# Moving beta and g of a gated delta rule into the feed-forward stage, and its closing norms into the rule's schedule

## The chip, the cores and the metric

The kernel runs on one core of a Trainium2 chip. The metric is the device time of one execution in microseconds (us); where several executions were timed, their median is given. Profiles are of one execution each. Engine names: PE is TensorE (matmuls; PEld its weight loads), DVE is VectorE, ACT is ScalarE, POOL is GpSimd, SP is SyncE, which issues most DMA transfers here.

## The reference, cut to what matters

The program is a decoder of two layers on 2048 tokens (32 sequences of 64, 256 features), all in float32: retention-like attention, banded cross attention, a feed-forward, then a gated delta rule, cross attention, and a mixture of 64 experts. A layer norm follows each. The change lies at the feed-forward of the first layer and the delta rule behind it:

```python
y = square(relu(x @ up)) @ down + (x @ expert) * sum_of_top2(x @ gate)
x = layernorm(x + layernorm(y) * gamma + beta)                    # feed-forward

beta = sigmoid(x @ w_b)                                           # [tokens, 32 heads]
g = -exp(a_log) * softplus(x @ w_a + dt_bias)                     # [tokens, 32 heads]
g = cumsum(g within each sequence)
decay[i, j] = exp(g[i] - g[j]) for i >= j                          # per sequence and head
...                                                               # the rule, 16 key heads, 32 value heads
x = layernorm(x + rule(x, beta, decay) @ w_out)
```

beta and g depend on nothing but the x that leaves the feed-forward.

## The kernel before, in words

The tokens are 16 tiles of 128, held in SBUF as `x[:, t, :]` throughout, and worked in four chunks of four tiles (512 tokens). One stage follows another; each has its own pools, and a tool that builds the program interleaves the instructions of neighbouring stages on each engine where their dependences let it.

The feed-forward (lines 662 to 708) is a plain loop over the four chunks. For a chunk it transposes x (`make_xT`, line 152: 8 transposes into two PSUM banks, two copies on ACT, L161), multiplies by the up weights in 8 blocks (`ph`, L678), takes relu on ACT (`hr`, L682, two buffers) and squares on POOL (`hT`, L683), then for each of the four tiles multiplies by the expert and gate weights (`pe`, L689) and the down weights (`py`, L692), and adds them on DVE (L694 to L700). Then a norm of y, the scaling on POOL (L705, L706), the addition to x (L707), and a norm of x (`layernorm`, L163: statistics on DVE, the power on POOL, four DVE operations L176). All PSUM tiles of the stage share one ring of 8 banks.

The delta rule's stage (from line 711) first loads constants by SP's queue (L718 to L760), among them two zero fills of the DRAM buffers `tudram` (L755, 1040 KB each, from a zeroed tile). It transposes x again for all four chunks (L742). Then it computes beta and g for all 16 tiles at once (lines 762 to 806): `pba` is x times w_b and w_a (L770, two groups of 8 tiles), ACT and DVE turn it into beta (exp, add, reciprocal) and into g (abs, exp, Ln, and three DVE operations), `pc` is the cumulative sum by a triangular matrix `tri` (L791, to `gall`), `pgT` the same transposed (L798), copied by ACT and stored by 16 DMA transfers to `gdram` (L804). The tiles of this part lie in a pool of their own, whose space the rule's working tiles take over.

The rule then has 64 steps, one for each of 16 key heads and 4 chunks: `conv` (projection `pp` L850, and a convolution over time on DVE, L859), `decay` for two steps (reloads g from `gdram` by a broadcast, L873; POOL subtracts, L884, L885; ACT exp, L888), `matrices` (`pn` L910, `pk` L943, stores to `adram` L957, and a reload `w` L964), `invert` (a triangular inverse on DVE, L1007, through `tudram`), `delta`, `gate` (`pz` L1047), `value` (`pv` L985), `output`, and `project` (L1158 to L1169), which adds to x.

Their order is not written by hand. Each of these is a Python generator, which yields steps such as `("pe", 1.75, "+")`: an engine, an estimated cost in us, and how many PSUM banks it takes (`+`) or gives back (`-`). `scheduled` (line 41) runs all streams in a model of the engines while the program is being built, and always emits next the step that can start first, with the streams' rank deciding among near equals. `("need", key)` holds a generator until another one has yielded `("set", key)`, which may add a latency. Streams come with the number of their items that may be under way. The emitted order is then fixed: on the chip each engine takes its instructions strictly in that order and waits on semaphores.

After the schedule four norms follow (lines 1199 to 1206), each with a store of its chunk of x to `xq`, from which the next stage, the second cross attention, loads its queries (`quarters`, L593).

Of the kernel before, what the change touches and what calls it, by code (L numbers as in the profile page):

```python
# [9 lines left out]
FP = mybir.dt.float32  # L10
# [8 lines left out]
P = 128  # L19
# [101 lines left out]
def decoder_kernel(ctx: ExitStack, tc: tile.TileContext, d, out):  # L121
# [537 lines left out]
        softmax_attention(wp, sb, ps, prologue, epilogue, True)  # L659


    with tc.tile_pool(name="f0", bufs=1) as wp, tc.tile_pool(name="f0w", bufs=2) as sb, tc.tile_pool(
        name="f0p", bufs=8, space=PSUM
    ) as ps:
# [7 lines left out]
        for c in range(NCH):  # L672
            make_xT(c, ps)
            hT = sb.tile([P, 8, 512], FP, name="hT", tag="hT")
            for f in range(8):
                ph = ps.tile([P, 512], FP, name="ph", tag="ps")
                for k in range(2):
                    nc.tensor.matmul(  # L678
                        ph, up[:, k, f * P : (f + 1) * P], xT[c][:, k, :], start=k == 0, stop=k == 1
                    )  # L680
                hr = sb.tile([P, 512], FP, name="hr", tag="hr")
                nc.scalar.activation(hr, ph, AF.Relu)  # L682
                nc.gpsimd.tensor_tensor(hT[:, f, :], hr, hr, ALU.mult)  # L683
            ys = []
            for k4 in range(4):
                cols = slice(k4 * P, (k4 + 1) * P)
                pe = ps.tile([P, D + 8], FP, name="pe", tag="ps")
                for k in range(2):
                    nc.tensor.matmul(pe, xT[c][:, k, cols], eg[:, k, :], start=k == 0, stop=k == 1)  # L689
                py = ps.tile([P, D], FP, name="py", tag="ps")  # L690
                for f in range(8):
                    nc.tensor.matmul(py, hT[:, f, cols], down[:, f, :], start=f == 0, stop=f == 7)  # L692
                m8 = sb.tile([P, 8], FP, name="m8", tag="m8")
                nc.vector.max(out=m8, in_=pe[:, D : D + 8])  # L694
                sc = sb.tile([P, 1], FP, name="sc", tag="sc")
                nc.vector.tensor_tensor(sc, m8[:, 0:1], m8[:, 1:2], ALU.add)
                ye = sb.tile([P, D], FP, name="ye", tag="ye")
                nc.scalar.activation(ye, pe[:, :D], AF.Copy, scale=sc)
                y = sb.tile([P, D], FP, name="y", tag=f"y{k4}")
                nc.vector.tensor_tensor(y, py, ye, ALU.add)  # L700
                ys.append(y)
            layernorm(ys, ys)
            tiles = [x[:, 4 * c + k4, :] for k4 in range(4)]
            for xt, y in zip(tiles, ys):
                nc.gpsimd.tensor_tensor(y, y, gam, ALU.mult)  # L705
                nc.gpsimd.tensor_tensor(y, y, bet, ALU.add)  # L706
                nc.vector.tensor_tensor(xt, xt, y, ALU.add)  # L707
            layernorm(tiles, tiles)


    with tc.tile_pool(name="g1", bufs=1) as wp, tc.tile_pool(
# [12 lines left out]
        PITCH = 65 * S  # L724
        adram = [dp.tile([2, 2, 8, PITCH], FP, name=f"adram{i}") for i in range(2)]
        tudram = [dp.tile([2, 2, 2, 8, PITCH], FP, name=f"tudram{i}") for i in range(2)]
        gdram = dp.tile([16, NCH, 2, 4, 2, S], FP, name="gdram")
        gall = wp.tile([P, NT, 32], FP, name="gall")

        wo16 = [wp.tile([P, 2, 16, 16], FP, name=f"wo16{i}") for i in range(2)]  # L730
        xis = [[wp.tile([P, 8, S], FP, name=f"xi{l}{i}") for i in range(2)] for l in range(2)]
# [7 lines left out]
        half = wp.tile([P, 4], FP, name="half")  # L739
        nc.gpsimd.memset(half, 0.5)  # L740

        for c in range(NCH):  # L742
            make_xT(c, ps)


        beta = wp.tile([P, NT, 32], FP, name="beta")
        with tc.tile_pool(name="g1l", bufs=1) as tmp:
            lvlf = load(tmp, d["c_lvl"].rearrange("p (l i) -> p l i", l=2), [P, 2, S], "lvlf")
            nc.vector.tensor_copy(lvl, lvlf)
# [4 lines left out]
            for t in tudram:  # L754
                nc.sync.dma_start(  # L755
                    out=t.rearrange("o c n u x -> (o c n u x)").rearrange("(p y) -> p y", p=P), in_=zero
                )
            tri = load(tmp, d["c_tri"], [P, P], "tri")
            wba = load(tmp, d["w_ba"].rearrange("(k p) e -> p k e", p=P), [P, 2, 64], "wba")
            dtb = load(tmp, d["dt_bias"].to_broadcast([P, 32]), [P, 32], "dtb")  # L760
            alog = load(tmp, d["a_log"].to_broadcast([P, 32]), [P, 32], "alog")
            g = tmp.tile([P, NT, 32], FP, name="g")
            aa = tmp.tile([P, NT, 32], FP, name="aa")
            ab = tmp.tile([P, NT, 32], FP, name="ab")
            for t8 in range(2):
                pba = ps.tile([P, 8, 64], FP, name="pba", tag="ps")
                for k8 in range(8):
                    t = 8 * t8 + k8
                    for k in range(2):
                        nc.tensor.matmul(  # L770
                            pba[:, k8, :], xT[t // 4][:, k, (t % 4) * P : (t % 4 + 1) * P], wba[:, k, :],
                            start=k == 0, stop=k == 1,
                        )
                sl = slice(8 * t8, 8 * t8 + 8)
                nc.scalar.activation(beta[:, sl, :], pba[:, :, 0:32], AF.Exp, scale=-1.0)
                nc.vector.tensor_tensor(aa[:, sl, :], pba[:, :, 32:64], over(dtb, 8), ALU.add)
            nc.vector.tensor_scalar(beta, beta, 1.0, None, ALU.add)
            nc.vector.reciprocal(beta, beta)
            nc.scalar.activation(alog, alog, AF.Exp)
            nc.scalar.activation(ab, aa, AF.Abs)  # L780
            nc.scalar.activation(ab, ab, AF.Exp, scale=-1.0)
            nc.scalar.activation(ab, ab, AF.Ln, bias=1.0)
            nc.vector.scalar_tensor_tensor(ab, aa, 0.0, ab, ALU.max, ALU.add)

            for hh in range(2):
                nc.vector.scalar_tensor_tensor(
                    g[:, :, 16 * hh : 16 * hh + 16], ab[:, :, hh::2], -1.0, over(alog[:, hh::2], NT),
                    ALU.mult, ALU.mult,
                )
            pc = pstile("pc")  # L790
            nc.tensor.matmul(pc, tri, g.rearrange("p t h -> p (t h)"), start=True, stop=True)  # L791
            nc.vector.tensor_copy(gall.rearrange("p t h -> p (t h)"), pc)

            gT = tmp.tile([32, NCH, 4, 2, S], FP, name="gTall")
            for c in range(NCH):
                pt = ps.tile([32, 4, P], FP, name="pgT", tag="ps")
                for k4 in range(4):
                    nc.tensor.matmul(  # L798
                        pt[:, k4, :], g[:, 4 * c + k4, :], tri, start=True, stop=True
                    )  # L800
                nc.scalar.copy(gT[:, c].rearrange("h t n i -> h (t n i)"), pt.rearrange("h t i -> h (t i)"))
                for n in range(2):
                    for hh in range(2):
                        nc.sync.dma_start(  # L804
                            out=gdram[:, c, n, :, hh, :], in_=gT[16 * hh : 16 * hh + 16, c, :, n, :]
                        )

        sb = stage.enter_context(tc.tile_pool(name="g1w", bufs=2))
        wsrc = d["w_qkv"].rearrange("(k p) e -> p k e", p=P)
# [21 lines left out]
        def conv(s, i):  # L831
# [3 lines left out]
            if i == first:  # L835
                yield "need", ("done", s - (5 if i == 2 or c == 0 else 6))
                yield "need", ("value" if i else "matrices", s - 2)
                if i == c == 0:
                    load_weights(kh)
                name = "vv" if i else "kq"  # L840
                projected[s, i] = sb.tile([P, 2, 512], FP, name=name, tag=name)
                yield "set", ("begun", s, i)
            else:
                yield "need", ("begun", s, first)
            dst = projected[s, first][:, 1 - i if i < 2 else i - 2]
            ct = (kh, 16 + kh, 32 + 2 * kh, 33 + 2 * kh)[i]
            yield "pe", 1.75, "+c"
# [19 lines left out]
        def decay(m):  # L867

            kh, c0 = steps[2 * m]
            yield "need", ("matrices", 2 * m - 3)  # L870
            de = sb.tile([P, 2, 8, S], FP, name="de", tag="de")
            for n in range(2):
                nc.sync.dma_start(  # L873
# [161 lines left out]
        def gate(s, h):  # L1035

            kh, c = steps[s]
            if h == 0:
                yield "need", ("done", s - 3)
                gates[s] = sb.tile([P, 2, 512], FP, name="z", tag="z", bufs=3)  # L1040
            yield "pe", 1.75, "+"
            if h == c == 0:
# [131 lines left out]
        def convs():  # L1174

            for m in range(-2, NS // 2):
# [3 lines left out]
                for s in (2 * m + 4, 2 * m + 5):  # L1180
                    if s < NS:
                        yield from (conv(s, 0), conv(s, 1))

        each = range(NS)
        scheduled(
            [
                ((output(s) for s in each), 1),
                ((matrices(s) for s in each), 2),
                ((value(s) for s in each), 1),
# [3 lines left out]
                (convs(), 2),  # L1193
                ((gate(s, h) for s in each for h in range(2)), 1),
                ((invert(m) for m in range(NS // 2)), 1),
            ],
            (6, 2), [(key, s) for s in range(-8, 0) for key in ("done", "matrices", "value", "output")],
        )
        for c in range(NCH):
            tiles = [x[:, 4 * c + k4, :] for k4 in range(4)]  # L1200
            layernorm(tiles, tiles)
            nc.sync.dma_start(
                out=xq[4 * c * P : (4 * c + 4) * P, :].rearrange("(t p) f -> p t f", p=P),
                in_=x[:, 4 * c : 4 * c + 4, :],
            )


    with tc.tile_pool(name="x1", bufs=1) as wp, tc.tile_pool(name="x1w", bufs=2) as sb, tc.tile_pool(
# [305 lines left out]
```

## Time and profile before

| what | us |
|---|---|
| median of 7 executions | 3573.0 |
| lowest and highest of them | 3568.04, 3584.35 |
| profiled execution, its own time | 3581.11 |
| its span, first to last instruction | 3579.4 |
| PE busy | 3311.9 (93%) |
| DVE busy | 2104.2 (59%) |
| POOL busy | 1525.2 (43%) |
| ACT busy | 1381.8 (39%) |
| feed-forward, first up matmul | 739.40 |
| the rule, first projection | 933.44 |
| the rule, last addition to x | 2597.75 |

The profile gives, for one execution, each engine's busy time, a strip of 40 slices of the span with the busy share in tenths, the granted clock of TensorE, and tables of instructions. In a row of the timeline the first number is the start in us from the beginning of the span, the second the length of a run of like instructions, then engine, line, operation, and what it writes and reads; `x32` is a count. A matmul of float32 appears as two passes, a transpose as one. In square brackets stands how long the engine had been idle and what ended it. "SPq" rows are DMA issues on SP's queue; they show the issue, not the transfer.

### The profile page before, as it was taken

What the parts mean: (1) busy time and instruction counts of PE and PEld (TensorE: products, weight loads), DVE (VectorE), ACT (ScalarE), POOL (GpSimd) and SP (SyncE); (2) the same over time, 40 slices, a digit from 0 to 9 for tenths busy, and PEclk for the clock granted to TensorE, in tenths of its full rate; (3) what the DMA queues carried; (4) which work ended last, traced back from release to release, by engine and by line L of the source; (5) the groups of instructions that cost most, each with busy time, mean ns of one, the idle gap of its engine ahead of it and who ended that gap; (6) DMA issues with size and microseconds to landing.
All of it is one profiled execution on the core that took longest, in us unless ns stands there. A gap on an engine that the chain in (4) does not pass through costs nothing.

```text
span 3579.4 us, 91942 instructions
## 1 busy us (share of the span) xinstructions
PE 3311.9 (93%) x39042; PEld 2137.0 (60%) x39042; DVE 2104.2 (59%) x4316; ACT 1381.8 (39%) x2422; POOL 1525.2 (43%) x1779
## 2 busy tenths in 40 slices
PE   9999999988799999999999999999979999699990
PEld 4667566655466666666676666666745555355550
DVE  4333566535476667777677677777567766233337
ACT  1110233322444455555455555555423333233330
POOL 3222344435334434444444444444334544466663
PEclk9999999999799999999899999999989998899995
DMA  9910111001242223323333233332221111466655
GB/s 313 384 49 13 43 31 31 27 31 38 52 78 55 57 55 70 64 55 57 62 60 66 57 67 63 62 59 48 46 49 53 63 49 41 163 220 211 214 176 217
DMA packets 538699, 317.80 MB, mean 89 GB/s; under 512 B 420144, under 2 KB 498736, under 8 KB 531888
## 3 DMA queue, kind: packets, MB, share of 16 engines
q1 hardware_dynamic: 517680, 259.32, 27.9%
q0 software_dynamic: 18432, 50.49, 3.9%
q8 instruction: 308, 5.05, 0.6%
q10 hardware_dynamic: 2176, 2.10, 0.2%
q14 instruction: 103, 0.84, 0.1%
HBM read 166.42 MB, written 137.00 MB: 85 GB/s over the span
## 4 chain that ended last, share of the span: by engine, by line
PE 77%; DVE 9%; POOL 5%; issue 4%; ACT 3%; DMA 1%; SPq 1%; POOLq 0%; DVEq 0%; ACTq 0%
PE pp L850 11%; PE py L1158 6%; PE po L531 6%; PE pz L1047 5%; PE pq L296 4%; PE pm L1067 4%; PE sc L467 3%; PE po L1118 3%; PE px L1067 3%; PE py L384 3%; PE sc L499 3%; PE py L1372 3%; PE pg L1362 2%; PE pu L1362 2%; PE ptu L1067 2%
## 5 line engine op out<-in xcount | busy, mean ns | idle before, releaser
L859 DVE SCALAR_TENSOR_TENSOR acc<-pp,cw,acc 128x504 f32<-128x504 f32 (+2 forms) x768 | 556.8, 731 | 195.2 <-ACT acc L854 165.3
L850 PE MATMUL pp<-xT,wqkv 128*128 128x512 f32 x1024 | 506.1, 620 | 22.5 <-DMA wqkv<-in_w_qkv_dram 11.7
L509 ACT ACTIVATE eT<-sc 128x768 f32<-128x768 f32 (+1 forms) x256 | 220.8, 914 | 265.7 <-PE sc L499 265.7
L903 POOL TENSOR_TENSOR sq<-kq 128x512 f32<-128x512 f32 x128 | 134.2, 1050 | 440.8 <-ACT kq L864 336.1
L204 POOL DMA_INDIRECT ybuf<-ye,xe x256 | 245.6, 959 | 176.8 <-DVE ye L1376 96.6
L477 DVE TENSOR_REDUCE mext<-sc 128x4 f32<-128x768 f32 (+1 forms) x256 | 267.3, 1087 | 73.1 <-PE sc L467 72.8
L850 PEld LDWEIGHTS pp<-xT,wqkv 128*128 128x128 f32 x1024 | 185.6, 194 | 185.1 <-issue 167.6
L1169 POOL TENSOR_TENSOR x<-x,y 128x256 f32<-128x256 f32 x256 | 184.2, 726 | 254.2 <-DVE x L1167 247.5
L854 ACT ACTIVATE acc<-pp,cw 128x512 f32<-128x512 f32 x256 | 175.2, 686 | 237.0 <-PE pp L850 236.3
L1158 PE MATMUL py<-wo,og 128*128 128x256 f32 x1024 | 259.2, 392 | 2.4 <-DVE x L1167 2.4
L1047 PE MATMUL pz<-xT,wz 128*128 128x512 f32 x512 | 246.2, 602 | 0.0
L518 POOL TENSOR_SCALAR_AFFINE_SELECT eT<-eT 128x256 f32<-128x256 f32 (+1 forms) x256 | 127.2, 531 | 201.3 <-ACT eT L509 201.3
L1158 PEld LDWEIGHTS py<-wo,og 128*128 128x128 f32 x1024 | 186.4, 192 | 43.6 <-issue 16.7
L467 PE MATMUL sc<-k,q 32*128 32x192 f32 (+1 forms) x2048 | 198.6, 397 | 10.6 <-DMA q<-xq 6.8
L1365 DVE TENSOR_TENSOR hT<-hT,pu 96x512 f32<-96x512 f32 x64 | 43.7, 683 | 238.1 <-PE pu L1362 221.9
L1167 DVE SCALAR_TENSOR_TENSOR x<-py,ro,x 128x256 f32<-128x256 f32 x256 | 122.4, 480 | 93.2 <-ACT y L1165 91.1
L499 PE MATMUL sc<-qb,k 32*128 32x192 f32 (+1 forms) x2048 | 160.5, 379 | 13.2 <-DVE mext L477 10.0
L1144 POOL TENSOR_TENSOR ro<-gvar,mhalf 128x8 f32<-128x8 f32 x64 | 105.2, 1644 | 147.5 <-DVE gvar L1139 137.8
L1165 ACT ACTIVATE y<-py,ro 128x256 f32<-128x256 f32 x256 | 120.4, 473 | 110.6 <-PE py L1158 101.6
L531 PE MATMUL po<-eT,va 128*32 128x192 f32 (+1 forms) x2048 | 159.9, 382 | 3.3 <-ACT eT L509 2.1
L298 DVE TENSOR_TENSOR tmp<-pq,cs 128x1024 f32<-128x1024 f32 x80 | 98.0, 1225 | 98.7 <-PE pq L296 93.9
L467 PEld LDWEIGHTS sc<-k,q 32*128 32x128 f32 x2048 | 116.2, 192 | 65.8 <-issue 36.2
(226 smaller groups left out, 6558.9 us busy)
## 6 DMA issues: line engine op xcount, KB each, us to landing
xbuf<-zero SPq DMA_DIRECT2D x32, 1032.0 KB
xe<-xbuf SPq DMA_DIRECT2D x64, 516.0 KB
tu<-tudram SPq DMA_DIRECT2D x256, 128.0 KB
ybuf<-zero SPq DMA_DIRECT2D x16, 1024.0 KB
de<-gdram SPq DMA_DIRECT2D x64, 256.0 KB
adram<-am SPq DMA_DIRECT2D x128, 128.0 KB
yk<-ybuf SPq DMA_DIRECT2D x16, 1024.0 KB
kk<-kT SPq DMA_DIRECT2D x32, 256.0 KB
```

Of the source, the lines that this page charges most:

```text
L204: i = nc.gpsimd.indirect_dma_start(out=dst, out_offset=bass.IndirectOffsetOnAxis(ap=rows, axis=0), in_=src, in_offset=None).ins
L467: nc.tensor.matmul(sc[ng // 2][:, ng % 2, qt * W : (qt + 1) * W], q32[rows, r, qt * P : (qt + 1) * P], k32[rows, r, lo[qt] : lo[qt] + W], ...
L477: nc.vector.tensor_reduce(mv4[:, 2 * hf : 2 * hf + 2, :, 8], sc[hf][:, :, : 2 * W].rearrange("p j (q l) -> p j q l", l=W), AX.X, ALU.max, ...
L499: nc.tensor.matmul(sc[ng // 2][:, ng % 2, lt * W : (lt + 1) * W], k32[rows, r, lt * P : (lt + 1) * P], qb[rows, lo[lt] : lo[lt] + W], star ...
L509: nc.scalar.activation(eT[:, 2 * hf : 2 * hf + 2].rearrange("p j h q -> p j (h q)"), sc[hf][:, :, : 2 * W], AF.Exp, scale=float(1 / np.sqr ...
L531: nc.tensor.matmul(po[32 * ng : 32 * ng + 32, i, lo[lt] : lo[lt] + W], one8[:, r, :] if i else va[:, lt, ng, 32 * r : 32 * r + 32], eT[:, ...
L850: nc.tensor.matmul(pp, weights[kh][0][:, k, i, :], xT[c][:, k, :], start=k == 0, stop=k == 1)
L859: nc.vector.scalar_tensor_tensor(acc3[:, :, sh:], pp3[:, :, : S - sh], w[:, 3 - sh : 4 - sh], acc3[:, :, sh:], ALU.mult, ALU.add,)
L1047: nc.tensor.matmul(pz, weights[kh][1][:, k, h * P : (h + 1) * P], xT[c][:, k, :], start=k == 0, stop=k == 1)
L1067: nc.tensor.matmul(dst[n, u], lhsT[n, u], rhs[n, u], start=True, stop=True)
L1158: nc.tensor.matmul(py[:, h, :], og[:, 4 * h + t].rearrange("p n i -> p (n i)"), won[:, h, :], start=True, stop=True,)
L1169: nc.gpsimd.tensor_tensor(xt, xt, y1, ALU.add)
```

## The change

1. A pool that lives from the feed-forward to the end of the rule holds `gall`, `beta`, `tri`, `wba`, `dtb`, `alog` and `gdram`. Their four loads stand ahead of the feed-forward's own, and alog's exp behind them.
2. `betas(c)` does for one chunk what the old code did for all: transposes, pba, beta, g, cumulative sum, its transposed form, and four stores. In the feed-forward it is run out for chunk c-1 between the up matmuls and the first `pe` of chunk c. The last chunk's runs as a stream of the rule's schedule.
3. The rule's streams need `("xT", c)` and `("g", c)`, which for chunks 0 to 2 are known from the start.
4. The old preparation is gone. `close(c)` puts the closing norm and the store of a chunk into the schedule as one more stream, at the last rank.

```diff
+    early = ctx.enter_context(ExitStack())
+    gp = early.enter_context(tc.tile_pool(name="gp", bufs=1))
+    gd = early.enter_context(tc.tile_pool(name="gd", bufs=1, space=bass.MemoryType.DRAM))
+    gdram = gd.tile([16, NCH, 2, 4, 2, S], FP, name="gdram")
+    gall = gp.tile([P, NT, 32], FP, name="gall")
+    beta = gp.tile([P, NT, 32], FP, name="beta")
+    tri = load(gp, d["c_tri"], [P, P], "tri")
+    wba = load(gp, d["w_ba"].rearrange("(k p) e -> p k e", p=P), [P, 2, 64], "wba")
+    dtb = load(gp, d["dt_bias"].to_broadcast([P, 32]), [P, 32], "dtb")
+    alog = load(gp, d["a_log"].to_broadcast([P, 32]), [P, 32], "alog")
+    nc.scalar.activation(alog, alog, AF.Exp)
+    def betas(c, ps):
+        xT[c] = xpool.tile([P, 2, 512], FP, name=f"xT{c}", tag=f"xT{c}")
+        for half in range(2):
+            yield "pe", 0.45, "+"
+            pt = ps.tile([P, 512], FP, name="pt", tag="ps")
+            for k in range(4):
+                nc.tensor.transpose(
+                    pt[:, k * P : (k + 1) * P], x[:, 4 * c + k, half * P : (half + 1) * P], ident
+                )
+            yield "act", 0.6, "-"
+            nc.scalar.copy(xT[c][:, half, :], pt)
+        yield "set", ("xT", c)
+        sl = slice(4 * c, 4 * c + 4)
...
+        yield "pe", 1.0, "+"
+        pba = ps.tile([P, 4, 64], FP, name="pba", tag="ps")
+        for k4 in range(4):
+            for k in range(2):
+                nc.tensor.matmul(
+                    pba[:, k4, :], xT[c][:, k, k4 * P : (k4 + 1) * P], wba[:, k, :], start=k == 0, stop=k == 1
+                )
+        yield "act", 1.6
+        nc.scalar.activation(beta[:, sl, :], pba[:, :, 0:32], AF.Exp, scale=-1.0)
+        yield "dve", 0.3, "-"
+        aa, ab, g = row("aa"), row("ab"), row("g")
+        nc.vector.tensor_tensor(aa, pba[:, :, 32:64], over(dtb, 4), ALU.add)
+        yield "dve", 1.3
+        nc.vector.tensor_scalar(beta[:, sl, :], beta[:, sl, :], 1.0, None, ALU.add)
+        nc.vector.reciprocal(beta[:, sl, :], beta[:, sl, :])
+        yield "act", 3.5
+        nc.scalar.activation(ab, aa, AF.Abs)
+        nc.scalar.activation(ab, ab, AF.Exp, scale=-1.0)
+        nc.scalar.activation(ab, ab, AF.Ln, bias=1.0)
+        yield "dve", 0.8
+        nc.vector.scalar_tensor_tensor(ab, aa, 0.0, ab, ALU.max, ALU.add)
+        for hh in range(2):
+            nc.vector.scalar_tensor_tensor(
+                g[:, :, 16 * hh : 16 * hh + 16], ab[:, :, hh::2], -1.0, over(alog[:, hh::2], 4), ALU.mult, ALU.mult
+            )
+        yield "pe", 1.3, "++"
+        pc = ps.tile([P, 4, 32], FP, name="pcum", tag="ps")
+        nc.tensor.matmul(
+            pc.rearrange("p t h -> p (t h)"), tri, g.rearrange("p t h -> p (t h)"), start=True, stop=True
+        )
+        pt = ps.tile([32, 4, P], FP, name="pgT", tag="ps")
+        for k4 in range(4):
+            nc.tensor.matmul(pt[:, k4, :], g[:, k4, :], tri, start=True, stop=True)
+        yield "dve", 0.3, "-"
+        nc.vector.tensor_copy(gall[:, sl, :], pc)
+        yield "act", 0.6, "-"
+        gT = gp.tile([32, 4, 2, S], FP, name="gT", tag="gT")
+        nc.scalar.copy(gT.rearrange("h t n i -> h (t n i)"), pt.rearrange("h t i -> h (t i)"))
+        for n in range(2):
+            for hh in range(2):
+                nc.sync.dma_start(out=gdram[:, c, n, :, hh, :], in_=gT[16 * hh : 16 * hh + 16, :, n, :])
+        yield "set", ("g", c), 3.0
...
                 nc.gpsimd.tensor_tensor(hT[:, f, :], hr, hr, ALU.mult)
+            if c:
+                for _ in betas(c - 1, ps):
+                    pass
             ys = []
...
-        for c in range(NCH):
-            make_xT(c, ps)
...
-            tri = load(tmp, d["c_tri"], [P, P], "tri")
...
-            for t8 in range(2):
-                pba = ps.tile([P, 8, 64], FP, name="pba", tag="ps")
...
-            gT = tmp.tile([32, NCH, 4, 2, S], FP, name="gTall")
...
+            yield "need", ("xT", c)
             dst = projected[s, first][:, 1 - i if i < 2 else i - 2]
...
             yield "need", ("matrices", 2 * m - 3)
+            yield "need", ("g", c0 + 1)
...
+        def close(c):
+            yield "need", ("done", NS - NCH + c)
+            tiles = [x[:, 4 * c + k4, :] for k4 in range(4)]
+            mv = small.tile([P, 4, 2], FP, name="mv4", tag="mv")
+            for i, xt in enumerate(tiles):
+                yield "dve", 0.65
+                st = small.tile([P, 6], FP, name="st", tag="st")
+                nc.vector.bn_stats(out=st, in_=xt)
+                nc.vector.bn_aggr(out=mv[:, i, :], in_=st)
...
+            nc.sync.dma_start(
+                out=xq[4 * c * P : (4 * c + 4) * P, :].rearrange("(t p) f -> p t f", p=P),
+                in_=x[:, 4 * c : 4 * c + 4, :],
+            )
...
         scheduled(
             [
+                (iter([betas(NCH - 1, ps)]), 1),
                 ((output(s) for s in each), 1),
...
                 ((invert(m) for m in range(NS // 2)), 1),
+                ((close(c) for c in range(NCH)), 1),
             ],
-            (6, 2), [(key, s) for s in range(-8, 0) for key in ("done", "matrices", "value", "output")],
+            (6, 2),
+            [(key, s) for s in range(-8, 0) for key in ("done", "matrices", "value", "output")]
+            + [(key, c) for c in range(NCH - 1) for key in ("xT", "g")],
         )
-        for c in range(NCH):
-            tiles = [x[:, 4 * c + k4, :] for k4 in range(4)]
-            layernorm(tiles, tiles)
...
+    early.close()
```

## The prediction

> **What bounds the kernel now.** I read the page first (busy time, then the 40 slices), then the timeline of TensorE from 725 to 960 us, the other engines over the same stretch, and the busy time and granted clock by stage. The page says that TensorE carries the program, and that it is missing in one place ahead of the long middle stage:
>
> ```profile
> span 3579.4 us, 91942 instructions
> PE   9999999988799999999999999999979999699990
> ```
>
> Slices are 89.5 us; the 7 is the feed-forward's end and the delta rule's preparation. The timeline of TensorE (start, length, line, operation, idle time before it) shows one feed-forward chunk and then that gap:
>
> ```profile
> 773.50 14.00 PE L678 MATMUL ph<-xT,up 128*128 128x512 f32 x32 [0.24 <-ACT xT L161]
> 787.34 1.05 PE L689 MATMUL pe<-eg,xT 128*128 128x264 f32 x4
> ...
> 868.55 3.62 PE L692 MATMUL py<-down,hT 128*128 128x256 f32 x16
> 872.75 2.84 PE L158 MATMUL pt<-ident,x 128*128 128x128 f32 x24 [0.59 <-DVE y L700]
> 885.89 2.45 PE L158 MATMUL pt<-ident,x 128*128 128x128 f32 x8 [10.30 <-DVE x L176]
> 894.20 13.89 PE L770 MATMUL pba<-wba,xT 128*128 128x64 f32 x64 [5.86 <-issue]
> 914.12 2.05 PE L791 MATMUL pc<-g,tri 128*128 128x512 f32 x2 [6.04 <-issue]
> 916.10 5.67 PE L798 MATMUL pgT<-tri,g 128*32 128x128 f32 x32
> 933.44 5.57 PE L850 MATMUL pp<-xT,wqkv 128*128 128x512 f32 x8 [11.67 <-DMA wqkv<-in_w_qkv_dram]
> ```
>
> So 61.2 us pass from the last down matmul (ending about 872.2) to the rule's first projection (933.44): the chunk's norms, beta and g of all tokens, the store of g and the loads behind it. Inside the feed-forward TensorE is never idle over 0.3 us in a chunk: what is put in line there is paid in full. The clock in the two places, from the busy time by stretch (last three columns: granted clock, DMA share, GB/s):
>
> ```profile
> 772.00:805.00 33.00, 32.47 (x120) 21.76 (x119) 17.85 (x42) 7.75 (x14) 16.58 (x18) 1.00 0.00 1
> 890.00:908.00 18.00, 13.80 (x64) 13.73 (x64) 0.42 (x1) 0.61 (x2) 0.00 (x0) 0.50 0.18 67
> ```
>
> **The change, part by part.** The changed kernel's instruction order, engine by engine, is what I price it by.
>
> *1. beta and g inside the feed-forward (three chunks).* After the ph matmuls of chunk c TensorE now has, in this order and with nothing between: 8 transposes of chunk c-1, 16 passes of pba, pcum, 8 passes of pgT, and only then pe. Each waits for the one before it through ScalarE and VectorE. In chunk 1:
>
> ```profile
> 785.65 6.22 POOL L683 TENSOR_TENSOR hT<-hr 128x512 f32<-128x512 f32 x6
> 785.72 4.26 DVE L176 TENSOR_SCALAR x<-x,mv,rstd 128x256 f32<-128x256 f32 x4 [1.14 <-POOL rstd L174]
> ...
> 789.86 0.60 ACT L682 ACTIVATE hr<-ph 128x512 f32<-128x512 f32 x1 [0.45 <-POOL hT L683]
> ```
>
> The order of these rows on their engines does not change. TensorE is free at 787.34, but the previous chunk's norm, which the transposes read, ends at 789.98: 2.6 us. ScalarE is in its relus until 790.46, then does the two copies (L161: 1.07 us for two), until 791.55: 1.6 us. Then pba: transposes at full clock take 0.109 us each (8 in 0.87 us), pba passes at half clock 0.217 (64 in 13.89), so 14 passes still to do and 0.2 us of latency are 1.75 us at full clock, 3.2 at half. Then the chain from pba to g, which took 6.0 us (908.10 to 914.12) on tiles two and four times as wide:
>
> ```profile
> 908.12 0.38 ACT L775 ACTIVATE beta<-pba 128x256 f32<-128x256 f32 x1 [6.44 <-PE pba L770]
> 908.53 0.42 DVE L776 TENSOR_TENSOR aa<-pba,dtb 128x256 f32<-128x256 f32 x1 [6.40 <-ACT beta L775]
> ...
> 910.30 1.28 ACT L782 ACT_TABLE_LOAD   x1
> 911.60 0.63 ACT L782 ACTIVATE ab<-ab 128x512 f32<-128x512 f32 x1
> ```
>
> Between the 0.23 us of 32 elements (L779) and the 0.63 of 512, 128 elements cost ScalarE about 0.3; VectorE's 0.42 at 256 becomes 0.29. So exp 0.3, aa 0.3, abs 0.35, exp 0.35, table load 1.3, Ln 0.3, three VectorE operations 0.7, handovers 0.25: 3.85 us. The reciprocal, 3.35 us on 512, is 0.85 on 128 and falls under the table load. A second table load (back to Exp) stands ahead of the first exp in chunks 2 and 3; it waits for nothing and runs under pba. Last pcum and pgT: 1.0 us at full clock, 1.9 at half (5.67 us for 32 passes). Sum from 787.34 to pe: 2.6 + 1.6 + 1.75 + 3.85 + 1.0 = 10.8 us; with the clock down throughout, 13.2. If it fell, the restart is slow too: the first ph block after a gap took 15.62 us against 14.00, 1.6 more. And 0.3 us that pe/py now wait for hT (791.93) go. Bounds for a chunk 10.5 and 14.5. TensorE has two stretches of 2.6 and 3.9 us with next to no work in 10 us; at 726.6 to 729.5 the granted clock went to half after 2.9 us of idle. I take 13.5, near the upper end: **+40.5 us** for three (31.5 to 43.5). No cover exists: the engine that waits is the bound.
>
> The Trainium skill, "ScalarE: Activation LUTs", What ACT_TABLE_LOAD costs, gives a load with its drain 2.66 us. Here Ln starts 0.02 us behind a 1.28 us load; by the page each chunk would be 1.4 us longer and the sum 4 us higher. I go by the row.
>
> The Trainium skill, "TensorE: Matmul & The Clock Gate", Part 1, shows a re-throttle 5.2 us after the last matmul. By that, no gap here would lower the clock, and a chunk would be at its lower bound. The rows above (2.9 us) speak against it, and the sum does not use it.
>
> *2. Four loads ahead of the up weights.* tri, wba, dtb and alog now stand on SP's queue before up, for which TensorE waits 3.41 us at 739.40. The loads there take 0.4 to 0.6 us each to issue, 160 KB in all. The same four took 1.16 to 1.27 us each at 886. So 1.5 to 5; I take **+1.9 us**, since the queue of transfers is short there. alog's exp is ahead of the first relu on ScalarE, and its load lands before ph is done: nothing.
>
> *3. The rule's start.* Gone from the gap: the three hidden transposes' copies, 64 pba passes of which 16 stay, the chain, 32 pgT passes, 16 stores of g ahead of the weights. What is late next? The norms of the last chunk still end at 887.6 and TensorE still waits for them (transposes first in its order); pba of the last chunk, at half clock 3.5 us, ends about 893. But the weights are later. SP issues the two zero fills (2.1 MB) at 885.28, and the first reload of g waits for their landing, because its tile takes over the space of theirs; wqkv is behind that reload. DMA ran at 433 GB/s until 892, at 163 until 894 and then at 2, and the pba that waited for a load behind the fills started at 894.20. So the reload is issued at about 893.4. In the old order it went at 927.62, and the first pp came 5.8 us after it:
>
> ```profile
> 885.28 0.84 SPq L755 DMA_DIRECT2D tudram<-zero  x2
> 927.62 1.30 SPq L873 DMA_DIRECT2D de<-gdram  x2
> ```
>
> First pp at 899.2 instead of 933.44: **-34 us** (33 to 35). The decay's subtraction on POOL and its exp come as long after the reload as before. The last chunk's chain (ScalarE 893 to 896) lies under the reload.
>
> *4. The last chunk in the schedule.* pcum and pgT (1 us) go between the first pk and the third pz; the stores of g's last chunk then precede adram on SP, and the second reload follows them. TensorE is full for the first 38 us of the rule, so its order counts: pk of step 1 comes after 16 pp and 12 pz matmuls instead of 14 and 10, with 8 transposes also moved ahead, some 5 us later. adram, the load of w and the inversion hang on it (w issued at 965.62, first use 971.51 on VectorE, delta at 1011.42). VectorE has two more conv operations ahead of the inversion to fill part of it. Bounds: -2 (the schedule gains) and +6; I take **+3 us**, nearer the 5 us shift. From there on all engines have the old order.
>
> *5. The norms as a stream.* In the order of every engine the end of the rule is what it was: two xq stores together, the third after gw, the fourth after two k loads; the VectorE and POOL rows match one for one, their waits too. **0 us**: the old program had already been interleaved there (an L176 at 2569.89 beside the last L1167 rows).
>
> **Sum.** 40.5 + 1.9 - 34 + 3 = **+11.4 us**. The profiled execution was 3581.11 us, span 3579.4, and stands 8.1 us above the median of seven (3573.0); no step depends on that offset. 3573.0 + 11.4 = 3584.4.
>
> **Rivals.**
> - *The clock holds and the start's order costs nothing.* pba and the transposes then count as work enough: 3 x 10.5 + 1.9 - 34 + 0 = -0.6 us, 3572.4. For it: only the 3.9 us stretch is wholly idle. Against: 2.9 us sufficed at 729.5.
> - *The rule starts as soon as its inputs allow* (the other side: not slower). If the reload does not wait for the fills, wqkv goes out at about 887.5 and pp starts when pba ends, 893: the saving is 40.5. With the chunks at 11.5, 34.5 + 1.9 - 40.5 + 0 = -4 us, 3569. It decides as soon as three chunks cost under 38.6 us. Against: the reload's listed waits name the fills' queues.
> - *The chain is longer still.* Half clock all through, slow loads, the late inversion: 43.5 + 5 - 33 + 6 = +21.5 us, 3594.5.
> - *The change does not do what it says* holds for its last part only, and is in the sum at 0.
>
> **How the numbers follow.** About 0.2% (7.1 us) is what a measurement of this kernel can tell from no change. Forecast (+5 to +17): 0.56; clock holds: 0.18; early start: 0.10; longer chain: 0.16. The range takes in the longer chain and most of the first rival, and, on both ends, a few us for the scatter of medians: 3569 to 3598. Slower: the forecast's part above 7.1 us (0.48) and the longer chain: 0.64. Within: the rest of the forecast (0.08), the clock rival but for a slip to either side (0.14) and most of the early start (0.06): 0.28. Faster: 0.08.
>
> **What would show it.** In the changed profile each of three feed-forward chunks should be 47 us long instead of 33.3, pe starting 11 to 13 us after the last ph, with clock digits under full speed there; the first pp 27 us after the last py; first delta matmuls 78 to 84 us after it; from 2570 us on, shifted by the sum, the same rows. It is wrong if TensorE's wait for g in a chunk is under 9 us or the first pp comes before 22 us.

## The result, and the profile after

The changed kernel takes 3601.0 us (median of 19 runs, 3591.16 to 3611.72) beside 3575.39 (46 runs of the kernel before, 3564.67 to 3594.22): ratio 1.0074, 95% interval 1.0064 to 1.0083. That is 25.6 us more, where 11.4 were forecast, and 3 us above the end of the range. The profiled execution took 3613.35 us (span 3611.6), 12 us above its median; that of before stood 6 to 8 above.

Two rows of the strip, of the page of after. A slice is 90.3 us here.

```profile
PE   9999899988789999999999999999979999699990
PEclk9999999988888999999899999999989999799995
```

Before, one 7 marked the preparation. Now there are five slices of granted clock at 8, from the feed-forward to well inside the rule; in the last of them, from 1083.5 us, PE is back at 9 and the clock is not, so part of the loss is busy time at a lower clock. TensorE's timeline of chunk 1, from the ph block that stood at 773.50 before:

```profile
776.93 14.00 PE L754 MATMUL ph<-xT,up 128*128 128x512 f32 x32 [0.24 <-ACT xT L161]
...
793.46 0.77 PE L681 MATMUL pt<-ident,x 128*128 128x128 f32 x5 [0.72 <-DVE x L176]
794.46 3.74 PE L696 MATMUL pba<-wba,xT 128*128 128x64 f32 x16 [0.24 <-ACT xT L685]
801.92 0.80 PE L721 MATMUL pcum<-g,tri 128*128 128x128 f32 x2 [3.72 <-DVE g L715]
...
804.49 2.13 PE L768 MATMUL pe<-eg,xT 128*128 128x264 f32 x4
```

TensorE waits for the norm until 793.46 and for g until 801.92. pe takes 2.13 us where it took 1.05 before: the granted clock is at half from 794.36 to 808.01. The chain in the second wait is the one priced before: pba ends at 798.2, the exp of beta begins at 798.24, the table load of 1.28 us at 799.54, Ln at 800.83.

And TensorE's waits in the whole feed-forward (total, count, longest):

```profile
PE pcum L721 <- DVE g L715: 11.2, 3, 3.7
PE pt L681 <- DVE x L176: 5.3, 9, 0.7
```

The gap ahead of the rule, TensorE, and then SP's queue:

```profile
933.36 2.87 PE L681 MATMUL pt<-ident,x 128*128 128x128 f32 x8 [13.73 <-DVE x L176]
...
946.90 3.75 PE L874 MATMUL pp<-xT,wqkv 128*128 128x512 f32 x4 [6.75 <-issue]
```

```profile
941.19 1.30 SPq L898 DMA_DIRECT2D de<-gdram  x2
```

The first pp comes 27.3 us after the last py (919.63) instead of 61.3, the reload of g about 8 us behind the fills (issued at 932.95): this part went as written.

The two executions, laid on each other at marks (add n: the n-th addition to x on POOL in the rule, counted from 0). "Step" is what the stretch up to the mark added; "at half clock" is the time in it with a granted clock of 0.50.

| mark | before | after | step | at half clock, before and after |
|---|---|---|---|---|
| first ph | 739.40 | 742.40 | +3.0 | |
| last py ends | 872.16 | 919.63 | +44.5 | 3.3, 45.1 |
| first pp | 933.44 | 946.90 | -34.0 | 47.4, 22.8 |
| first px of a delta | 1011.42 | 1029.46 | +4.6 | 14.1, 14.7 |
| add 4 | 1050.35 | 1072.03 | +3.6 | 0.4, 6.8 |
| add 8 | 1073.69 | 1106.47 | +11.1 | 3.0, 30.7 |
| add 64 | 1452.41 | 1481.25 | -3.9 | 30.6, 20.5 |
| end | 3579.39 | 3611.64 | +3.4 | |

So there is a loss of 15.4 us between the first pp and add 64 that nothing in the forecast but a +3 stands for, and 11.1 us of it are one stretch, from add 4 to add 8, with 30.7 us at half clock. TensorE's timeline there, in after:

```profile
1068.06 1.88 PE L874 MATMUL pp<-xT,wqkv 128*128 128x512 f32 x4
1072.49 1.12 PE L1093 MATMUL ptu<-xi,tu 64*64 64x32 f32 x32 [2.55 <-issue]
1073.41 0.28 PE L1093 MATMUL px<-tu,am 64*64 64x32 f32 x2
1073.62 1.49 PE L874 MATMUL pp<-xT,wqkv 128*128 128x512 f32 x2
1075.04 1.92 PE L1093 MATMUL px<-tu,am 64*64 64x32 f32 x32
```

and the same place in before (rows not shown so far):

```profile
1044.75 1.11 PE L1067 MATMUL px<-tu,am 64*64 64x32 f32 x30
1048.27 1.13 PE L1158 MATMUL py<-wo,og 128*128 128x256 f32 x4 [2.40 <-DVE x L1167]
...
1049.76 3.67 PE L850 MATMUL pp<-xT,wqkv 128*128 128x512 f32 x4
1053.37 1.06 PE L1067 MATMUL ptu<-xi,tu 64*64 64x32 f32 x29
```

Both stand idle for about 2.5 us and both lose the clock behind it. In before, four passes of pp fill the next 3.7 us, and the 32-column ptu is back at 1.06 us for 29. In after the same four passes have been issued ahead of the idle time, and two others follow it; px, which in before takes 1.11 us for 30 passes at 1044.75, takes 1.92 for 32, and so on to 1104.97. The busy time by stretch of after (length, PE busy first; granted clock, DMA share, GB/s last) says it in one row:

```profile
1074.30:1104.90 30.60, 30.60 (x370) 24.11 (x369) 10.23 (x25) 8.30 (x15) 4.45 (x4) 0.50 0.25 44
```

TensorE is busy for all of the 30.6 us, and the clock stays at 0.50.

### The profile page after: what moved, and what is told of

Its sections match the earlier page's. It is cut to its first block, busy times and chain, and to the rows that moved or that the text cites. A ratio compares the mean times of both kernels' runs of the same rounds, so it can differ in the third digit from the quotient of the medians.

```text
span 3611.6 us, 91980 instructions
## 1 busy us (share of the span) xinstructions
PE 3336.2 (92%) x39048; PEld 2150.6 (60%) x39048; DVE 2104.8 (58%) x4336; ACT 1391.9 (39%) x2439; POOL 1524.4 (42%) x1779
## 4 chain that ended last, share of the span: by engine, by line
PE 78%; DVE 9%; POOL 4%; issue 3%; ACT 3%; DMA 1%; SPq 0%; POOLq 0%; DVEq 0%; ACTq 0%
PE pp L874 11%; PE py L1184 6%; PE po L531 6%; PE pz L1073 5%; PE pq L296 4%; PE pm L1093 4%; PE sc L467 3%; PE px L1093 3%; PE po L1144 3%; PE py L1420 3%; PE py L384 3%; PE sc L499 3%; PE pg L1410 3%; PE pu L1410 3%; PE ptu L1093 2%
## 5 line engine op out<-in xcount | busy, mean ns | idle before, releaser
L1093 PEld LDWEIGHTS px<-tu,am 64*64 64x64 f32 x4096 | 137.1, 141 | 35.7 <-issue 23.0
```

What stands on the lines that cost most here:

```text
L1093: nc.tensor.matmul(dst[n, u], lhsT[n, u], rhs[n, u], start=True, stop=True)
```

## The experiments

Three theories stood at the start. By T1 the loss is made of waits in the feed-forward and the half clock that follows from them, of late loads, and of about 5 us for the last chunk in the schedule; the long half clock in the rule's start is chance. By T2 that half clock belongs to the schedule's order with the last chunk in it and comes in every run. By T3 the norms as a stream cost something. Kernels sent together ran on one chip with the kernel before, whose median was 3578.9 us in the first four, 3681.0 in the second and 3692.8 in the third. The 100 us more of the last two lie behind the rule (from its last addition to x to the first pg, a matmul of the mixture of experts, 590 us instead of 490, in the changed kernel as it is); so times are compared as ratios, and stretches up to add 64 in us.

**e1_norms.** The kernel before with the last part alone.

```diff
+        def close(c):
+            yield "need", ("done", NS - NCH + c)
...
+                ((close(c) for c in range(NCH)), 1),
...
-        for c in range(NCH):
-            tiles = [x[:, 4 * c + k4, :] for k4 in range(4)]
-            layernorm(tiles, tiles)
```

> The kernel before with the last part of the change alone: the norms at the rule's end as a stream of its schedule. T1 (the feed-forward's waits, the late loads and the last chunk in the schedule make up the whole difference; the norms nothing): 3575 us, within 3 us of the kernel before, ratio 0.999 to 1.001. T3 (the stream of norms costs time at the rule's end): 4 to 12 us slower, ratio 1.001 to 1.0035.

Measured: 1.0004 (0.9989 to 1.0019). The interval alone would leave room for the low end of T3. The profiles do not: from add 240 to the end of add 255 both kernels take 37.9 us, and the first matmul sc of the next stage comes 14.0 us (before) and 14.1 us (e1) behind it. T3 falls; the norms' stream is worth nothing either way.

**e6_spread.** The same steps behind the pe/py groups.

```diff
-            if c:
-                for _ in betas(c - 1, ps):
-                    pass
+            steps = betas(c - 1, ps) if c else iter(())
+            next(steps, None)
...
             for k4 in range(4):
                 cols = slice(k4 * P, (k4 + 1) * P)
+                for step in steps if k4 else ():
+                    if step[:2] in (("pe", 1.0), ("pe", 1.3)):
+                        break
...
+            for _ in steps:
+                pass
```

> The changed kernel with the steps of a chunk's beta and g put between the four pe/py groups of the feed-forward's chunk, so that each wait of the chain lies behind a group of matmuls; the same instructions, in another order. T1 (the 14.7 us by which each chunk grew are TensorE's waits in its own order, and the half clock that follows from them): only TensorE's own work stays, 0.9 for the transposes, 1.75 for pba and 1.0 for pcum and pgT at full clock, 3.6 us a chunk; 3 x 11 = 33 us less: 3568 us, ratio 0.998; some 5 us more if the chain's instructions delay ScalarE's ye. Rival (the chain's instructions on ScalarE and VectorE cost the time by themselves, wherever they stand): not more than 12 us less, 3589. Rival (the clock falls in the rule's start whatever the feed-forward does): as T1.

Measured: 0.9985 (0.9972 to 0.9998), 0.0089 or 32 us less than the changed kernel. Its timeline of TensorE in chunk 1, and its busy time by stretch there:

```profile
802.01 1.89 PE L696 MATMUL pba<-wba,xT 128*128 128x64 f32 x16
...
809.44 1.16 PE L770 MATMUL pe<-eg,xT 128*128 128x264 f32 x4
```

```profile
774.00:815.00 41.00, 40.39 (x175) 28.68 (x173) 21.20 (x51) 12.61 (x24) 16.58 (x18) 1.00 0.01 2
```

No wait and full clock: the stretch from the first ph to the last py is 146.1 us, 13.3 above before, 4.4 a chunk. That is TensorE's own work for beta and g; the other 10.4 us a chunk were order: waits, and the half clock behind them. In the rule's start the 30.7 us at half clock are there again.

**e5_filler.** Work for TensorE where it waits, to part the clock from the waits.

```diff
+                for step in betas(c - 1, ps):
+                    if step[:2] in (("pe", 0.45), ("pe", 1.3)) and step not in fed:
+                        fed.append(step)
+                        for _ in range(4):
+                            fill = ps.tile([P, 512], FP, name="fill", tag="ps")
+                            for k in range(2):
+                                nc.tensor.matmul(fill, up[:, k, :P], xT[c][:, k, :], start=k == 0, stop=k == 1)
```

> The changed kernel with four pairs of matmuls (128 x 512, unread, 1.75 us at full clock) ahead of the transposes and four ahead of pcum in each of the three chunks, where TensorE waits: work added, output unchanged. T1 (of the 14.7 us of a chunk some 4 are the half clock that the two waits cause, the rest the waits): no or little half clock in the feed-forward instead of 41 us, pba 1.9 us instead of 3.74, the way from the last ph to the next pt 10.5 to 12 us instead of 14.7 above before, last py 8 to 12 us earlier. Rival (the 14.7 us are the chain's length whatever the clock): the stretch is unchanged within 1 us a chunk.

Measured (one execution): half clock in the feed-forward 6.1 us instead of 45.1, but the last py 8.3 us later, not earlier. The expectation had priced a filler at a quarter of its 16 passes: each took 7.0 us, not 1.75, and more than filled the waits:

```profile
790.48 7.03 PE L768 MATMUL fill<-xT,up 128*128 128x512 f32 x16
...
808.69 1.16 PE L774 MATMUL pe<-eg,xT 128*128 128x264 f32 x4
```

As a saving it failed; as a price list it serves. Against the rows of after: pba 3.74 to 1.89 (the row of e6_spread), pcum 0.80 to 0.38, pgT 1.92 to 1.06, pe 2.13 to 1.16, py 4.42 to 3.62: 4.9 us in this chunk are the clock. With 4.4 of work and 5.7 of waits (11.2 + 5.3 + 0.5 for pba, by three) that makes 15.0, and 14.8 were measured.

**e2_last_ahead.**

```diff
+        for _ in betas(NCH - 1, ps):
+            pass
         scheduled(
             [
-                (iter([betas(NCH - 1, ps)]), 1),
...
-            + [(key, c) for c in range(NCH - 1) for key in ("xT", "g")],
+            + [(key, c) for c in range(NCH) for key in ("xT", "g")],
```

> The changed kernel with the last chunk's beta and g run out ahead of the rule's schedule and not as a stream of it. T1 (the last chunk in the schedule costs some 5 us by its place in TensorE's order, and the drops of the clock in the rule's start are chance): the first pp comes some 7 us later, since SP's reload of g and wqkv now stand behind the store of the last g, and the first px after pp is back to 78 us from 82.6; together 0 to +4 us against the changed kernel's 3601: 3601 to 3605, ratio 1.0074 to 1.0085. T2 (the schedule's order with the last chunk in it lowers the clock in every run, and that is the 12 us that the sum lacks): 8 to 15 us less than the changed kernel in spite of the later pp: 3586 to 3593.

Measured: 1.0044 (1.0027 to 1.0062), 0.0030 or 11 us less than the changed kernel: T2's figure. The first pp came 34.9 us after the last py (+7.6), the first px 78.4 after that (-4.2), and add 4 to add 8 took 23.2 us with 2.5 at half clock. Its timeline has the order of before at that place, pp behind the idle time:

```profile
1069.36 1.13 PE L1184 MATMUL py<-wo,og 128*128 128x256 f32 x4 [2.23 <-DVE x L1193]
...
1070.98 3.45 PE L874 MATMUL pp<-xT,wqkv 128*128 128x512 f32 x4
```

**after_again.**

> The changed kernel once more as it is, for a second profile. The step at issue is the rule's second group of four adds to x (add 4 to add 8), 34.5 us in three profiles with the last chunk in the schedule (30.7 of them at half clock) and 23.3 in three without. T2 (the schedule's order lowers the clock there whenever it runs): again 34 us, and a time of 3600 us or more. T1 (chance): with this order too 23 to 27 us in some profiles.

Measured: 1.0072 (1.0044 to 1.0100); add 4 to add 8 35.3 us, 33.9 at half clock. Over all profiles of this study:

| kernels | add 4 to add 8 | of it at half clock |
|---|---|---|
| last chunk in the schedule: after (2 profiles), e4 (2), e5, e6 | 34.4 to 35.7 | 30.7 to 34.1 |
| last chunk not in it: before, e1, e2, e8 (2), e10 | 23.1 to 23.3 | 1.7 to 3.0 |

Six against six: T1's "chance" falls.

**e9_fill_idle and e11_fill_behind.** What lowers the clock, and what keeps it low. Filler in the idle time (e9), and behind it (e11):

```diff
             pt = units("ptu", 0)
+            for k in range(18 if s == 2 else 0):
+                nc.tensor.matmul(pt.rearrange("p u b c -> p (u b c)"), ident, xT[0][:, 0, :256], start=True, stop=True)
             per_sequence(pt, U, columns(xi[0], 0))
```

```diff
             px = units("px", 1)
+            for k in range(16 if s == 2 else 0):
+                nc.tensor.matmul(px.rearrange("p u b c -> p (u b c)"), ident, xT[0][:, 0, :256], start=True, stop=True)
             per_sequence(px, am, columns(T, 1))
```

> The changed kernel with 18 more matmuls (128 x 256, 4.2 us at full clock, their result overwritten unread) ahead of the first ptu of step 2, where TensorE stands idle for 2.55 us before the clock falls for 30.7 us. They add work and change no output. T2 with its mechanism (the idle time lowers the clock, and the 64-wide matmuls behind it are too little work to raise it again): no half clock from there on, add 4 to add 8 some 25 us instead of 34.5, and 7 to 9 us less than the changed kernel in the profile; ratio to the kernel before near 1.005. Rival (the fall has another cause than this idle time): the half clock stays and the time rises by 2 us, ratio 1.008.

> The changed kernel with 16 more matmuls (128 x 256, 3.8 us at full clock, 7.5 at half, overwritten unread) behind the idle 2.5 us and not in it: between the first ptu of step 2 and its second px. TensorE stands idle as before, only what follows differs. T2 with its mechanism (the 64-wide matmuls that follow are what keeps the clock at half once it has fallen; two stretches of dense work raise it): 3.4 to 10.2 us at half clock instead of 30.7 to 34.1, and add 4 to add 8 some 28 to 30 us instead of 34.5, in spite of the added work. Rival (the fall lasts 30 us whatever follows): some 30 us at half clock, add 4 to add 8 38 us or more.

e9 measured 1.0028 (1.0013 to 1.0043), e11 1.0030 (1.0013 to 1.0047): each about 16 us less than the changed kernel in spite of added work; of it 12.0 and 11.5 lie between the last py and add 64 (549.7 and 550.1 us against 561.6; the changed kernel's second profile has 567.5). A matmul is two passes here, so the fillers took twice what the expectations say (7.9 us in e9, 9.1 in e11). In e9 they fill the idle time and the place of pp, which moved behind ptu:

```profile
1065.13 7.93 PE L1115 MATMUL ptu<-xT,ident 128*128 128x256 f32 x36
1072.99 1.12 PE L1093 MATMUL ptu<-xi,tu 64*64 64x32 f32 x32
```

No half clock at all between add 4 and add 8. In e11 the idle time stays and the clock falls, for one stretch of 3.4 us only:

```profile
1070.90 1.12 PE L1093 MATMUL ptu<-xi,tu 64*64 64x32 f32 x32 [2.51 <-issue]
...
1072.03 4.54 PE L1120 MATMUL px<-xT,ident 128*128 128x256 f32 x12
1076.51 1.11 PE L1093 MATMUL px<-tu,am 64*64 64x32 f32 x30
```

So for this place both halves are shown: without the idle time the clock does not fall (e9), and dense matmuls behind it end the fall after one stretch of 3.4 us (e11). That 64-wide matmuls as such keep the clock low is not shown. In the profile of after, from 1087.91 to 1091.32, px and pm fill TensorE (3.41 us busy, clock 0.50), and the clock stays at 0.50 behind them; from 1248.33 to 1251.74 the same px and pm fill it (3.41 us busy, clock 0.50), and from 1251.75 the clock is 1.00. What decides between the two stays open.

**e4_loads_late and e4_again.**

```diff
-    tri = load(gp, d["c_tri"], [P, P], "tri")
-    wba = load(gp, d["w_ba"].rearrange("(k p) e -> p k e", p=P), [P, 2, 64], "wba")
...
         bet = load(wp, d["beta"].to_broadcast([P, D]), [P, D], "bet")
+        tri = load(gp, d["c_tri"], [P, P], "tri")
+        wba = load(gp, d["w_ba"].rearrange("(k p) e -> p k e", p=P), [P, 2, 64], "wba")
...
```

> The changed kernel with the four loads (tri, wba, dtb, alog) and the exp of alog behind the feed-forward's own loads. Both theories: the first ph comes 2.3 us earlier, as in the kernel before, and nothing else moves: 3598.5 us, ratio 1.0067. If the loads cost nothing (the wait for up is bound by something else): 3601. If the late wba or tri then holds up chunk 0's beta (needed some 45 us later, so not expected): more than 3601.

> The four loads behind the feed-forward's own, once more: the first time its profile had the first ph 2.9 us earlier and the last py 3.5, while its median was 9 us above the changed kernel's, with the intervals touching. If the loads cost what the profile shows: ratio 1.006 to 1.007. If moving them does harm that a single profile does not show: 1.009 again.

Measured: 1.0090 (1.0072 to 1.0107), then 1.0067 (1.0041 to 1.0094). First ph at 739.55 and 739.06. Over the profiles the loads ahead of up put it at 741.0 to 742.6, and behind it (or in the old place) at 739.1 to 739.7: 1.4 to 3.5 us. In the whole time that can't be told from nothing; why the first ratio came out 0.0016, some 6 us, above the changed kernel's stays open.

**e8_spread_ahead, e8_again and e10_late_loads.** e6_spread with the last chunk ahead of the schedule, its stores on ScalarE's queue; and the same with the loads late.

```diff
-                nc.sync.dma_start(out=gdram[:, c, n, :, hh, :], in_=gT[16 * hh : 16 * hh + 16, :, n, :])
+                (nc.scalar if c == NCH - 1 else nc.sync).dma_start(out=gdram[:, c, n, :, hh, :], in_=gT[16 * hh : 16 * hh + 16, :, n, :])
```

> The steps of beta and g spread between the pe/py groups as in e6_spread, and the last chunk's run out ahead of the rule's schedule with its four stores of g on ScalarE's queue instead of SP's, so that wqkv does not wait for them. Both theories: the first pp as in e6_spread (last py + 27 us), since pgT ends 946.3 in the order of e2_last_ahead against a first pp at 946.9; the first px 78 us behind it instead of 81.4 (-3.5). T2: no long half clock in the rule's start, 7 to 11 us less; together 3561 to 3566 us at a before of 3577, ratio 0.996 to 0.997. T1: only the 3.5 us, ratio 0.9975.

> e8_spread_ahead once more, beside the same with late loads: ratio 0.9957 within its interval, 0.994 to 0.9975; add 4 to add 8 again 23 us, without the long half clock.

> e8_spread_ahead with the four loads and the exp of alog behind the feed-forward's own loads. If the loads cost 2.5 to 3 us ahead of up: the first ph at 739.5, ratio lower than e8_again's by 0.0007, which is near what can be told apart. If they cost nothing: the same. T2: no long half clock in the rule's start.

Measured: 0.9957 (0.9941 to 0.9973), 0.9943 (0.9925 to 0.9961), 0.9942 (0.9922 to 0.9962): faster than before by 15 to 21 us (of 3575), and than the changed kernel by 42 to 47. No long half clock. One expectation failed: the first px came 83.0 to 85.1 us after pp, not 78. The second reload of g, which waits for the last chunk's stores, was issued 3.0 to 3.6 us after the first pp instead of 1.8 ahead of it; its exp came on ScalarE at 14.4 to 15.4 instead of 13.0, the conv row behind it that much later, and the first pk at 22.8 to 24.8 instead of 17.9. What would come of a reload that does not wait was not tried.

## Why the prediction was wrong

*1. beta and g in the feed-forward: right mechanism, sized 4 us too low.* The order of waits was as written, row by row: transposes held by the norm to 2.7 us after ph (2.6 worked out), 3.72 us for g (3.85 from pba's end), pba 3.74. The clock fell as pba began, in each chunk. The term mis-sized is the half clock: 4.9 us a chunk, where my 13.5 (of 10.5 to 14.5) held 4.0 at its upper end and I took a point below that end. Measured 14.8, in all +44.5 instead of +40.5, 1 us above the bound of 43.5. pe began 13.7 us after ph, against "11 to 13". "No cover exists" held for this order only: in e6 the same work cost 4.4 us a chunk. And the row that the clock was weighed by reads a little otherwise: in before the clock fell at 729.06, 2.4 us and not 2.9 into the idle time.

*2. The loads:* +3.0 in the profile where +1.9 was taken; within its bounds, and 1.4 to 3.5 over all profiles.

*3. The rule's start:* -34.0, as forecast, by the rows named: the reload waits for the fills, and the norms' end is not what is late. The rival of an early start is refuted by the same rows.

*4. The last chunk in the schedule is the step that failed.* "Bounds: -2 (the schedule gains) and +6; I take +3 us", and "From there on all engines have the old order". It cost 15.4 us up to add 64 (13.9 to 21.8 over the six profiles with that order), and the order was not the old one: it differed in what stands on either side of an idle time of 2.5 us. Only TensorE's order up to the first delta was priced, at the clock of before. e2, e9 and e11 show what stands in the step's place: about 11 us, between add 4 and add 8, lost to a half clock that falls with this idle time and that the small matmuls placed behind it did not end, where dense ones did. Of the rest of the 15.4, 4.6 lie ahead of the first px and 3.6 up to add 4, with 6.4 us more at half clock than before; 3.9 come back by add 64, with 10 us less. None of the rivals had it; "the chain is longer still" (+21.5) came near the time by other terms.

Its first part was right, size and link: pk of step 1 came 32.3 us after the first pp instead of 26.8, am behind it (it waited for pk), and px 4.6 later. In after, TensorE and VectorE:

```profile
979.15 1.10 PE L968 MATMUL pk<-kq 128*64 128x128 f32 x16
```

```profile
980.36 0.69 DVE L976 TENSOR_TENSOR am<-pk,de 128x512 f32<-128x512 f32 x1 [3.59 <-PE pk L968]
```

A second link lies close beside it, which I had not priced: the second reload of g, held by the last chunk's stores, goes out 19.9 us after pp where it had gone 1.8 ahead, and POOL's last operation on that de ends at 979.81, 0.4 us ahead of pk. Had pk kept its place, am could have come only that much earlier.

*5. The norms:* nothing, as forecast; e1 shows it.

With the measured terms the sum is 44.5 + 3.0 - 34.0 + 15.4 + 0 = 28.9 us beside 25.6 between the medians and 32.2 between the two profiled spans. Of the 17.5 us by which 11.4 is short of that, 12.4 are step 4, 4.0 step 1 and 1.1 step 2. The rest of the rule moves by a few us to either side: in this pair of profiles the difference changes by +2.7 us up to add 128, -0.2 up to add 192 and -1.4 up to add 255, and by +2.3 behind the rule.

The range failed with step 4 too: its bounds came from shifts in the order alone, and the clock was weighed only in the feed-forward, where the forecast had looked for it.

## What to carry to other kernels

Work put in line on the engine that bounds the kernel costs its waits in full, and the same work between groups of matmuls that don't depend on it only its own time: 4.4 us a chunk instead of 14.8. When a change reorders a stretch that has an idle time in it, look at what stands behind the idle time as well as at its length: dense matmuls there ended a fall of the clock after 3.4 us, and with small ones it lasted 30.7. And a schedule worked out by a program, when it takes one more stream, keeps its order nowhere for certain: compare the two orders beyond the first place where they agree again.

## What the runs showed of the hardware

The stretches at half clock in the fourteen profiles are whole multiples of 3.41 us: 3.41, 6.83, 10.24, 13.65 and 30.72 us are among them. The Trainium skill, "TensorE: Matmul & The Clock Gate", Part 1, What's actually happening, has a free-running window of 3413 ns, half clock after an idle one and full clock after one of sustained work. The length agrees. The rest goes further here: 2.2 to 2.55 us of idle time were enough to lower the clock. In the rule, over all profiles, 59 of the 60 idle times of 2 us or more that began at full clock had it fall by 3.41 us after their end, and 33 of 44 between 1.5 and 2 us.

In the long stretches of after, e4 and e6, eight windows in a row with TensorE busy throughout did not raise the clock (nine in after's second profile and in e5). They held small matmuls, with at most 2.5 us of 128-wide ones in a window (2.6 in after's second profile); the window behind them, 128-wide throughout, raised it. One window of mostly 128-wide passes raised it in before, e2 and e11 as well. But the share of 128-wide passes is not the whole rule: in after a window with 2.2 us of them, from 1033.29, raised the clock, and so did the one without any from 1248.33. What the clock goes by was not found.
